# Expert-row gathers of a decoder kernel: their DRAM view, what they wait for, and their place in a step

## The chip, the cores and the metric

The kernel runs on one core of a Trainium2 chip. The metric is the device time of one execution in microseconds (us); lower is better. Times of the kernel before are 1217.22, 1217.5 and 1214.28 us, median 1217.22 us.

## The reference

One decoder layer on x of shape (8, 512, 256), in float32: windowed self-attention with a residual, cross-attention to 64 context rows with a residual, and a last block of a small attention and a mixture of experts. Only the last block touches the change. Its attention runs over the batch of 8 (512 independent positions), and its experts are chosen by arg-max:

```python
def _moe(x, Wg, W1, b1, W2, b2):
    xf = x.reshape(S * B, D)                  # 4096 tokens, D = 256
    idx = jnp.argmax(xf @ Wg.T, axis=-1)      # one of E = 8 experts per token
    out = jnp.zeros_like(xf)
    for e in range(E):
        m = (idx == e)[:, None].astype(xf.dtype)
        h = jax.nn.relu(xf @ W1[e] + b1[e])   # DF = 1024
        out = out + m * (h @ W2[e] + b2[e])
    return out.reshape(S, B, D)
y = _layer_norm(x + _mha(x, ...), g1, be1)
z = _layer_norm(y + _moe(y, Wg, W1, b1, W2, b2), g2, be2)
return x + z
```

## The kernel before, in words

A first part (lines 196 to 692) does the two attentions batch by batch; it ends near 680 us of the profile and is not touched. The second part (from line 704) does the last block and has three kinds of work.

*Blocks.* 4096 tokens are cut into NBLK = 8 blocks of four groups of 128 tokens. `block_start` normalises a block and makes its q, k and v. `group` does the attention of one group: scores (L794, L805), their maximum on VectorE (L814), exponentials on ScalarE (L820), in its next step the reciprocal of the sums (L828, VectorE) and the scaling of the weights (L829, a 128x512 multiply on GpSimd), in the step after that four transposes of the scaled weights on TensorE (L834), then the product with the values (L841) and the projection (L190, L854). `block_end` normalises the block (L154 to L158, L167, L170), transposes it (L179), computes the expert logits (L871, L885), counts how many tokens each expert has seen (L905) and gives each token a row in a DRAM table, `rows_d`, of 8 x 4096 rows of 513 words: the expert's region and the token's rank in it (`sloti`, L911 to L929). Four indirect DMAs issued by GpSimd, one per group, scatter the block's rows there (L931), two in one step and two in the next.

*Tables.* `make_table` runs three times, after blocks 3, 5 and 7. From the counts it derives which full tiles of 128 rows of one expert exist by then: expert index (`eidx`) and source rows (`srci`) per tile. Table t0 holds tiles 0 to 8 (NT1 = 9), t1 tiles 9 to 16 (NT2 = 17), t2 tiles 17 to 38 (NT = 39). t0 takes rows of blocks 0 to 3 only, t1 of blocks 0 to 5, t2 of all.

*Expert tiles.* `expert_tile(i)` gathers 128 rows from `rows_d` by an indirect DMA of GpSimd into one of seven buffers `tb` (L1067; the first seven tiles clear their buffer first, L1064). A step later SyncE loads the expert's first weights, b1 and b2 (L1079, 1 MB, L1081, L1083). A step later the rows are transposed on TensorE (L1094; VectorE copies them out, L1096, and takes the token numbers, L1087), a step later comes the first matmul (L1105, 32 matmuls) with its relu (L1110, L1112) and two additions on GpSimd (L1116, L1117), a step later the second matmul (L1121, 16 matmuls), its statistics and a power on GpSimd (L1135), and a step later the last two VectorE operations (L1137, L1138) and the scatter of the result to the output (L1139, GpSimd). The weights go into buffers that blocks 2 to 5 used for the rows they scattered (tags y2 to y5), so the first loads into such a buffer wait for that block's scatters.

*What sets the order.* `in_steps` (line 70) runs all these works as generators, one piece of each per step, sorted by the rank that the piece before yielded (a new work has the rank with which it is entered): PREFIX 0, TURN 1, VALUES 2, SMALL 3, SCORES 4, OTHER 5, EXPS 6, LOADS 7; at equal rank the newest work comes first. `in_order` (line 51) then ties each of TensorE, VectorE, ScalarE and GpSimd to that order. Block n enters at step 4n and its `block_end` at step 4n + 15; its scatters are in steps 4n + 20 and 4n + 21. Tile i enters at step 34 + i with rank PREFIX, so its gather stands before the multiply L829 of that step, which belongs to a group's piece that also has rank PREFIX but is older. The tiles' transposes L1094 (rank TURN) open TensorE's part of step 36 + i; the group's transposes L834 (SMALL) follow.

*What waits for what.* Dependencies between DMAs and compute are found from the tensors that they name. `dram_disjoint_views` hands out views of one DRAM tensor that count as disjoint from each other, so scatters do not wait for one another. The gather names the whole of `rows_d`, which overlaps every view:

```python
group_rows = dram_disjoint_views(rows_d, NGRP)
...
out=group_rows[n * NG + g0 + g],   # a scatter writes its own view
...
in_=rows_d,                        # a gather reads the whole tensor
```

A gather therefore waits for every scatter that stands before it in the order, and a scatter waits for every gather that stands before it. Both kinds wait in GpSimd's own instruction stream, ahead of everything behind them there. GpSimd's DMAs share eight semaphores in turn, so a DMA also waits for the eighth one before it.

Of the kernel before, what the change touches and what calls it, by code (L numbers as in the profile page):

```python
# [27 lines left out]
NBLK = S // (GP * NG)  # L28
# [3 lines left out]
NGRP = S // GP  # L32
NT = (B * S + E * (P - 1)) // P
NB1, NB2 = 4, 6
# [5 lines left out]
PREFIX, TURN, VALUES, SMALL, SCORES, OTHER, EXPS, LOADS = range(8)  # L40
# [58 lines left out]
def decoder_kernel(ctx: ExitStack, tc: tile.TileContext, a: dict, out: bass.AP):  # L99
    nc = tc.nc  # L100
# [8 lines left out]

    rows_d = dram.tile([E * B * S, ROW], I32, name="rows_d")  # L110

    group_rows = dram_disjoint_views(rows_d, NGRP)
    tile_rows = dram_disjoint_views(out.rearrange("b s d -> (b s) d"), NT)

    cst = const.tile([P, C_N], F32, name="cst")
# [31 lines left out]
    def statistics(src):  # L147

        n = src.shape[1]
        st = small.tile([P, NG, 6], F32, tag="st")  # L150
        mv = small.tile([P, NG, 2], F32, tag="mv")
        rs = small.tile([P, NG], F32, tag="rs")
        for i in range(n):
            nc.vector.bn_stats(st[:, i, :], src[:, i, :])  # L154
        for i in range(n):
            nc.vector.bn_aggr(mv[:, i, :], st[:, i, :])
        nc.vector.tensor_scalar(rs[:, :n], mv[:, :n, 1], EPS, None, ALU.add)  # L157
        nc.gpsimd.tensor_tensor(rs[:, :n], rs[:, :n], nhalf[:, :n], ALU.pow)  # L158
        return mv, rs
# [36 lines left out]
    with ExitStack() as p1:  # L196
# [59 lines left out]
        def context_keys():  # L256
            for hf in range(2):
                ps = ps_m.tile([P, 512], F32, tag="m")
                project(ps, xwk, hf * P, ctxT)
                for r, mask in enumerate((mask_e, mask_o)):  # L260
                    nc.vector.tensor_scalar(
                        kc[:, hf, :, r, :],
                        ps.rearrange("p (b k) -> p b k", k=NKC),
                        xbk[:, hf : hf + 1],
                        mask,
                        ALU.add,
                        ALU.mult,
                    )
                yield

        def context_values(bs):
            for b in bs:
                ps = ps_m.tile([P, 512], F32, tag="m")
                for r in range(2):
                    heads = slice(r * HD, (r + 1) * HD)
                    for k in range(2):
                        nc.tensor.matmul(
                            ps[r * 64 : (r + 1) * 64, :P],
                            ctxT[:, k, b * NKC : (b + 1) * NKC],
                            xwv[:, k, :].rearrange("p (j d) -> p j d", d=2 * HD)[:, :, heads],  # L280
                            start=k == 0,
                            stop=k == 1,
                        )
                for r in range(2):
                    rows = slice(r * 64, (r + 1) * 64)
                    heads = slice(r * HD, (r + 1) * HD)
                    nc.vector.tensor_tensor(
                        vc[rows, b, :, heads],
                        ps[rows, :P].rearrange("p (j d) -> p j d", d=HD),
                        xbv[rows].rearrange("p (j d) -> p j d", d=2 * HD)[:, :, heads],  # L290
                        ALU.add,
                    )
                if b % 2:
                    yield
# [7 lines left out]
        rows = [slice(32 * j, 32 * j + 32) for j in range(4)]  # L302
# [375 lines left out]
        works = [(4, context_keys()), (6, context_values(range(B)))]  # L678
# [25 lines left out]
    with ExitStack() as p2:  # L704
# [151 lines left out]
        def block_end(n, g0, ng):  # L856

            yr = state[n]["yr"]
            y = yr[:, g0 : g0 + ng, :D]
            stats = statistics(y)  # L860
            yield
            normalised(y, y, *stats, g1, be1)
            yield
            yT = fx.tile([P, 2, NG * P], F32, tag="yT", bufs=1, name=f"fyT_{n}_{g0}")
            transposed(yT[:, :, : ng * P], y, ps_m)
            yield

            ps = ps_m.tile([P, P], F32, tag="m")
            for k in range(2):
                for g in range(ng):  # L870
                    nc.tensor.matmul(  # L871
                        ps[32 * g : 32 * g + 32, :],
                        wg[:, k, :],
                        yT[:, k, g * P : (g + 1) * P],
                        start=k == 0,
                        stop=k == 1,
                        skip_group_check=True,
                    )
            lT = fx.tile([P, P], F32, tag="lT", bufs=1, name=f"lT_{n}_{g0}")
            nr = 32 * ng  # L880
            nc.scalar.copy(lT[:nr], ps[:nr])
            yield

            pl = ps_m.tile([P, NG, 32], F32, tag="m")
            nc.tensor.transpose(  # L885
                pl.rearrange("p g e -> p (g e)")[:, :nr], lT[:nr], ident[:nr, :nr]
            )
            lg = pl[:, :ng, :E]
            top = small.tile([P, NG], F32, tag="top")
            rv = small.tile([P, NG, E], F32, tag="lg")  # L890
            mk = small.tile([P, NG, E], F32, tag="emk")
            for i in range(2):
                nc.vector.tensor_reduce(top[:, :ng], lg, AX.X, ALU.max)
                nc.vector.tensor_tensor(
                    mk[:, :ng], lg, top[:, :ng].unsqueeze(2).to_broadcast([P, ng, E]), ALU.is_equal
                )
                if i == 0:
                    rev = cst[:, C_REV : C_REV + E].unsqueeze(1).to_broadcast([P, ng, E])
                    nc.vector.tensor_tensor(rv[:, :ng], mk[:, :ng], rev, ALU.mult)
                    lg = rv[:, :ng]  # L900

            before = small.tile([P, NG + 1, E], F32, tag="seen", bufs=2, name=f"seen{n}_{g0}")
            nc.vector.tensor_copy(before[:, 0], seens[-1])
            for g in range(ng):
                nc.vector.tensor_tensor(before[:, g + 1], before[:, g], mk[:, g, :], ALU.add)  # L905
            seens.append(before[:, ng])
            yield

            pr = ps_m.tile([P, NG, E], F32, tag="m")
            for w, v in ((cst[:, C_LT : C_LT + P], mk), (ones, before)):  # L910
                nc.tensor.matmul(  # L911
                    pr[:, :ng].rearrange("p g e -> p (g e)"),
                    w,
                    v[:, :ng].rearrange("p g e -> p (g e)"),
                    start=v is mk,
                    stop=v is before,
                )
            rk = small.tile([P, NG, E], F32, tag="rk")
            nc.vector.tensor_tensor(
                rk[:, :ng],  # L920
                pr[:, :ng],
                cst[:, C_E4 : C_E4 + E].unsqueeze(1).to_broadcast([P, ng, E]),
                ALU.add,
            )
            nc.vector.tensor_tensor(rk[:, :ng], rk[:, :ng], mk[:, :ng], ALU.mult)
            slot = small.tile([P, NG], F32, tag="slot")
            nc.vector.tensor_reduce(slot[:, :ng], rk[:, :ng], AX.X, ALU.add)
            sloti = small.tile([P, NG], I32, tag="sloti")
            nc.vector.tensor_copy(sloti[:, :ng], slot[:, :ng])  # L929
            for g in range(ng):  # L930
                nc.gpsimd.indirect_dma_start(  # L931
                    out=group_rows[n * NG + g0 + g],
                    out_offset=bass.IndirectOffsetOnAxis(ap=sloti[:, g : g + 1], axis=0),
                    in_=yr[:, g0 + g, :].bitcast(I32),
                    in_offset=None,
                )
                if g == 1:
                    yield

# [7 lines left out]


        tables = []

        def table(name, cnt, op, n, base, ends):

# [100 lines left out]
        def expert_tile(i):  # L1053
# [3 lines left out]
            k = sum(i >= n for n in at) - 1  # L1057
            (eidx, srci, void), j = tables[k], i - at[k]
            if i < 7:
# [7 lines left out]
            nc.gpsimd.indirect_dma_start(  # L1067
                out=t.bitcast(I32),
                out_offset=None,
                in_=rows_d,  # L1070
                in_offset=bass.IndirectOffsetOnAxis(ap=srci[:, j : j + 1], axis=0),
                bounds_check=E * B * S - 1,
                oob_is_err=False,
            )
            yield LOADS
            e_sp = nc.sync.value_load(eidx[0:1, j : j + 1], min_val=0, max_val=E - 1)
            w1 = fy.tile([P, NG, ROW], F32, tag=f"y{2 + i % 3 if i < 7 else (2, 5, 3, 4)[i % 4 - 2]}", name=f"w1_{i}")
# [42 lines left out]
            for f in range(NFC):  # L1120
# [21 lines left out]
                in_=r,  # L1142
# [6 lines left out]
        works = [(9, expert_weights())]  # L1149
# [5 lines left out]
        for k, (nb, n) in enumerate(((NB1, NT1), (NB2, NT2 - NT1), (NBLK, NT - NT2))):  # L1155
            works.append((4 * nb + 16, make_table(f"t{k}", n, nb < NBLK)))
        for i in range(NT):
            works.append((4 * NB1 + 18 + i, expert_tile(i), PREFIX))
        with in_order(tc):
            in_steps(works)  # L1160

# [102 lines left out]
```

## Time and profile before

| | |
|---|---|
| median of three runs | 1217.22 us (1214.28 to 1217.5) |
| the profiled execution's own time | 1219.89 us |
| its span, first to last instruction | 1218.1 us |
| TensorE (PE) busy | 1100.2 us, 90% |
| VectorE (DVE) / ScalarE (ACT) / GpSimd (POOL) busy | 722.7 / 581.8 / 498.7 us |
| mean granted TensorE clock | 0.953 |
| chain that ended last | PE 64%, DVE 18%, ACT 8%, issue 3%, DMA 3%, POOL 3% |
| scatters into `rows_d` (L931) | 32, 780.2 to 1015.4 us, median 0.972 us of GpSimd each |
| gathers from `rows_d` (L1067) | 9 + 8 + 22, from 870.0, 951.2 and 1025.5 us, median about 1.07 us each |

The page is read in this order: busy time and clock by engine, the slices that show where an engine thins out, then the chain that ended last, and from there the waits and the timeline of the stretch in question. Times in a timeline are microseconds from the start of the span. A releaser is what ended an idle time; where a wait had several conditions it is the one that the profile saw last, so one whose engine had long been done stands for another, often a DMA.

### The profile page before, as it was taken

The page shows a single profiled execution, that of the slowest core. Times are in us where ns is not written, and L with a number is a line of the kernel's source. Part 1 is how long each engine was busy: PE and PEld are TensorE (multiplying, and loading weights), DVE is VectorE, ACT ScalarE, POOL GpSimd, SP SyncE. Part 2 cuts the span into 40 slices and gives each one's busy share as a digit, 9 for nine tenths or more (in the row PEclk, how much of TensorE's full clock was granted, in tenths as well). Part 3 has the DMA queues.
Part 4 walks back from the last instruction along what each step waited for, and adds up shares of the span by engine and source line. Part 5 has one row for each costly group of instructions (what it writes and reads, how often), then busy time and mean ns, then how long its engine had stood idle before and what let it go on. Part 6 is the DMA issues. An engine that isn't in the chain of part 4 may idle for free.

```text
span 1218.1 us, 24488 instructions
## 1 busy us (share of the span) xinstructions
PE 1100.2 (90%) x8900; PEld 793.9 (65%) x8900; DVE 722.7 (59%) x1830; ACT 581.8 (48%) x2037; POOL 498.7 (41%) x580
## 2 busy tenths in 40 slices
PE   6798998999989999899876699999789999999995
PEld 3455666566655666656553367766568988999994
DVE  2947758477584866848551336667547764544553
ACT  2866758576595765867701165555332111111110
POOL 2242524425244243431510233544455566555543
PEclk9997999999999999999987699999899989999998
DMA  5000001010010100100001760120345866666630
GB/s 192 1 1 5 7 1 45 1 40 6 1 45 2 39 6 11 35 2 27 2 18 46 209 204 1 36 70 36 137 131 193 274 215 196 225 195 204 213 128 7
DMA packets 60727, 97.66 MB, mean 80 GB/s; under 512 B 15930, under 2 KB 43965, under 8 KB 60608
## 3 DMA queue, kind: packets, MB, share of 16 engines
q1 hardware_dynamic: 53056, 75.08, 19.9%
q0 software_dynamic: 7552, 21.02, 5.0%
q8 instruction: 72, 1.18, 0.4%
q14 instruction: 47, 0.39, 0.1%
HBM read 81.12 MB, written 17.71 MB: 81 GB/s over the span
## 4 chain that ended last, share of the span: by engine, by line
PE 64%; DVE 18%; ACT 8%; issue 3%; DMA 3%; POOL 3%; SPq 0%; POOLq 0%; DVEq 0%
PE ps L185 12%; PE ps L190 11%; PE hps L1105 9%; PE ps L1121 9%; ACT s L449 5%; PE sc L402 2%; DVE nm L445 2%; DVE s L429 2%; PE xav L636 2%; DVE nm L578 2%; PE ps L179 2%; DMA rows_d<-y,sloti 2%; PE av L507 2%; PE ps L805 1%; DVE kg L362 1%
## 5 line engine op out<-in xcount | busy, mean ns | idle before, releaser
L449 ACT ACTIVATE s<-s,nm 128x144 f32<-128x144 f32 (+1 forms) x512 | 203.7, 408 | 11.4 <-DVE nm L445 11.4
L1110 ACT ACTIVATE h<-hps,b 128x128 f32<-128x128 f32 x156 | 44.6, 369 | 233.7 <-issue 188.6
L1105 PE MATMUL hps<-tT,w 128*128 128x128 f32 x1248 | 150.2, 280 | 0.7 <-issue 0.6
L1105 PEld LDWEIGHTS hps<-tT,w 128*128 128x128 f32 x1248 | 146.7, 196 | 2.0 <-issue 0.6
L1121 PE MATMUL ps<-w,h 128*128 x624 | 141.0, 379 | 0.0
L484 POOL TENSOR_TENSOR pc<-pT,cst 128x512 f32<-128x512 f32 x96 | 122.8, 1300 | 24.9 <-DVE pT L480 24.7
L1121 PEld LDWEIGHTS ps<-w,h 128*128 128x128 f32 x624 | 115.7, 190 | 14.1
L449 ACT ACTIVATION_READ_ACCUMULATOR s<-s,nm 128x1 f32 x512 | 100.8, 197 | 0.0
L460 POOL COPY rx<-s 128x128 f32<-128x128 f32 x48 | 14.7, 306 | 193.5 <-ACT s L449 193.5
L445 DVE TENSOR_REDUCE nm<-s 128x8 f32<-128x1152 f32 (+1 forms) x64 | 84.5, 1320 | 13.2 <-POOL s L438 9.4
L1112 DVE TENSOR_SCALAR h<-hps,b 128x128 f32<-128x128 f32 x156 | 43.9, 344 | 65.0 <-ACT h L1110 58.0
L402 PE MATMUL sc<-kz,qT 32*128 32x512 f32 (+1 forms) x512 | 76.1, 603 | 4.1 <-DVE s L421 3.0
L429 DVE COPY_PREDICATED s<-upto_q,sc 128x512 f32<-128x512 int32 x96 | 64.8, 729 | 24.6 <-ACT s L428 24.5
L478 PE MATMUL pt<-cst,s 128*128 128x128 f32 x512 | 72.4, 281 | 2.6 <-ACT pT L482 1.1
L158 POOL TENSOR_TENSOR rs<-rs,nhalf 128x4 f32<-128x4 f32 x32 | 33.4, 1043 | 95.5 <-DVE rs L157 95.4
L478 PEld LDWEIGHTS pt<-cst,s 128*128 128x128 f32 x512 | 60.5, 145 | 15.3 <-issue 7.1
L428 ACT COPY s<-sc 128x512 f32<-128x512 f32 x96 | 51.6, 590 | 37.6 <-PE sc L402 37.5
L185 PE MATMUL ps<-fxT,w_fwqkv 128*128 128x512 f32 x128 | 60.9, 621 | 0.0
L463 DVE RECIPROCAL rc<-sm 128x8 f32<-128x8 f32 x64 | 12.6, 197 | 80.8 <-ACT s L449 80.8
L185 PE MATMUL ps<-xT,w_wqkv 128*128 128x512 f32 x128 | 58.5, 599 | 0.0
L829 POOL TENSOR_TENSOR s<-s,sm 128x512 f32<-128x512 f32 x32 | 33.4, 1045 | 59.0 <-DVE sm L828 56.7
L1139 POOL DMA_INDIRECT out<-r,to x39 | 39.8, 1020 | 29.5 <-DVE r L1138 13.4
(241 smaller groups left out, 2297.7 us busy)
## 6 DMA issues: line engine op xcount, KB each, us to landing
w<-in_W SPq DMA_DIRECT2D x47, 1024.0 KB
b<-in_b SPq DMA_DIRECT2D x39, 128.0 KB
xb<-in_x SPq DMA_DIRECT2D x8, 512.0 KB
x2d<-xb SPq DMA_DIRECT2D x8, 512.0 KB
y<-x2d SPq DMA_DIRECT2D x32, 128.0 KB
mi<-in_mask SPq DMA_DIRECT2D x8, 128.0 KB
mj<-in_maskT SPq DMA_DIRECT2D x8, 128.0 KB
w_wqkv<-in_wqkv SPq DMA_DIRECT2D x1, 768.0 KB
```

The source lines that it names most:

```text
L185: nc.tensor.matmul(ps, w[:, k, o0 : o0 + P], xT[:, k, :], start=k == 0, stop=k == 1)
L190: nc.tensor.matmul(ps, xT[:, k, t0 : t0 + P], w[:, k, o0 : o0 + D], start=k == 0, stop=k == 1)
L402: nc.tensor.matmul(ps[j // 2][:, j % 2].rearrange("p r w k -> p r (w k)"), qT[rows[j], hf, q0 : q0 + P], kz[rows[j], hf, :, q0 + P - nw * ...
L428: nc.scalar.copy(s4, ps[jj][:, :, :, 0, :])
L429: nc.vector.copy_predicated(s4, upto_q.unsqueeze(1).unsqueeze(1).to_broadcast([P, 2, 2, P]), ps[jj][:, :, :, 1, :],)
L445: nc.vector.tensor_reduce(nm, s[:, :, :nk], AX.X, ALU.max, negate=True)
L449: nc.scalar.activation(s[:, h, :nk], s[:, h, :nk], AF.Exp, bias=nm[:, h : h + 1], accum_out=sm[:, h : h + 1],)
L478: nc.tensor.transpose(pt[:, h, :], s[:, 4 * jj + h, :P], ident)
L484: nc.gpsimd.tensor_tensor(pc[:, hs, :], pT[:, hs, :], upto_k.unsqueeze(1).to_broadcast([P, 4, P]), ALU.mult,)
L1105: nc.tensor.matmul(ps[:, f, :], w1[:, k, f * P : (f + 1) * P], tT[:, k, :], start=k == 0, stop=k == 1)
L1110: nc.scalar.activation(h[:, f, :], ps[:, f, :], AF.Relu, bias=b1[:, f : f + 1])
L1121: nc.tensor.matmul(ps, h[:, f, :], w2[:, bass.ds(e_pe, 1), f, :].rearrange("p o d -> p (o d)"), start=f == 0, stop=f == NFC - 1,)
```

## The change

The gathers get views of their own, one per tile, that count as disjoint from the scatters' views and from each other. What a gather has to wait for is then said by name: the first 16, 24 or 32 scatters for a tile of table t0, t1 or t2. The instruction list is searched for the scatter just issued, and its name kept. Tiles enter their first step with rank VALUES in place of PREFIX.

```diff
-    group_rows = dram_disjoint_views(rows_d, NGRP)
+    group_rows = dram_disjoint_views(rows_d, NGRP + NT)
...
                     in_=yr[:, g0 + g, :].bitcast(I32),
                     in_offset=None,
                 )
+                scatters.append(traced()[-1].name)
...
         tables = []
+        scatters = []
+
+        def traced():
+            return nc.cur_bb.bb.instructions
+
+        known = (4 * NB1, 4 * NB2, 4 * NBLK)
...
             nc.gpsimd.indirect_dma_start(
                 out=t.bitcast(I32),
                 out_offset=None,
-                in_=rows_d,
+                in_=group_rows[NGRP + i],
                 in_offset=bass.IndirectOffsetOnAxis(ap=srci[:, j : j + 1], axis=0),
...
             )
+            gather = traced()[-1]
+            for scatter in scatters[: known[k]]:
+                tc.add_manual_dep(
+                    gather,
+                    scatter,
+                    mybir.DependencyInfo(mybir.DependencyClass.Sync, mybir.DependencyReason.DATA),
+                    reason="rows",
+                )
             yield LOADS
...
         for i in range(NT):
-            works.append((4 * NB1 + 18 + i, expert_tile(i), PREFIX))
+            works.append((4 * NB1 + 18 + i, expert_tile(i), VALUES))
```

In the built programs TensorE, VectorE, ScalarE and SyncE have the same instructions in the same order before and after. GpSimd has the same instructions; in each of steps 34 to 39 (865 to 913 us of the profile) the multiply L829 stands ahead of the clearing of `tb` and the gather (tiles 0 to 5), where it stood behind them, and nothing else changes place. Of the conditions on GpSimd's instructions, the scatters lose the gathers and the gathers the scatters that their table does not count; what is left of that kind is the first gather of each table, which waits for the last scatters that it counts, and the turn of the eight semaphores.

## The prediction

> **What bounds the kernel now.** I read the waits of TensorE (PE) first, between 840 and 1030 us, the stretch in which blocks 4 to 7 and the first expert tiles run side by side. PE is 90% busy over the span, and after 1030 us a tile takes 7.25 us with no gap (L1094 at 1034.20, 1041.44, 1048.69 in its timeline), so a gain can only lie in this stretch. Columns: who waited, for whom, us in total, times, longest.
>
> ```profile
> PE pt L834 <- POOL s L829: 10.4, 3, 5.1
> PE pt L1094 <- DMA tb<-rows_d,t1srci: 5.2, 2, 2.6
> ```
>
> PE waits for GpSimd's multiply and for two gathers. GpSimd's timeline (start, length; idle before it and its releaser in brackets) says why the multiply and the gathers are late:
>
> ```profile
> 864.76 0.97 POOL L931 DMA_INDIRECT rows_d<-y,sloti  x1 [0.30 <-issue]
> 865.74 0.54 POOL L1064 MEMSET tb<- 128x513 f32 x1
> 870.00 1.07 POOL L1067 DMA_INDIRECT tb<-rows_d,t0srci  x1 [3.72 <-DMA rows_d<-y,sloti]
> 871.10 1.05 POOL L829 TENSOR_TENSOR s<-s,sm 128x512 f32<-128x512 f32 x1
> ...
> 894.77 1.05 POOL L1067 DMA_INDIRECT tb<-rows_d,t0srci  x1 [4.23 <-DVE to L1087]
> ...
> 978.10 0.97 POOL L931 DMA_INDIRECT rows_d<-y,sloti  x1 [3.16 <-DMA tb<-rows_d,t1srci]
> ...
> 985.24 1.07 POOL L1067 DMA_INDIRECT tb<-rows_d,t1srci  x1 [2.94 <-DMA rows_d<-y,sloti]
> ```
>
> A multiply stands behind a gather that waits for scatters just issued; later, scatter waits for gather and gather for scatter, in turn. (The 4.23 us names VectorE, but this gather waits for the two scatters of 887.67 and 889.03; the second landed at 893.97 in the trace's semaphore records.) PE's timeline shows the four gaps:
>
> ```profile
> 872.20 1.11 PE L834 MATMUL pt<-cst,s 128*128 128x128 f32 x4 [5.08 <-POOL s L829]
> 896.95 1.11 PE L834 MATMUL pt<-cst,s 128*128 128x128 f32 x4 [4.46 <-POOL s L829]
> 989.17 0.66 PE L1094 MATMUL pt<-cst,tb 128*128 128x128 f32 x2 [2.63 <-DMA tb<-rows_d,t1srci]
> 1024.65 0.41 PE L1094 MATMUL pt<-cst,tb 128*128 128x128 f32 x2 [2.57 <-DMA tb<-rows_d,t1srci]
> 1025.46 5.44 PE L1105 MATMUL hps<-tT,w 128*128 128x128 f32 x32 [0.40 <-issue]
> ```
>
> Each gap has a second price. In the windows view (stretch, its us, busy us of PE, PEld, DVE, ACT, POOL, then clock, DMA share, GB/s) the clock is 0.50 after it:
>
> ```profile
> 869.20:872.60 3.40, 0.40 (x2) 0.40 (x3) 0.00 (x0) 0.00 (x0) 2.57 (x3) 0.50 0.55 180
> 872.60:876.05 3.45, 3.45 (x23) 2.15 (x22) 0.00 (x0) 2.17 (x10) 2.12 (x3) 0.50 0.86 319
> 893.10:896.50 3.40, 0.00 (x0) 0.00 (x0) 1.58 (x7) 0.35 (x2) 1.70 (x2) 1.00 0.00 0
> 896.50:899.94 3.44, 2.99 (x28) 2.04 (x28) 0.00 (x0) 1.31 (x5) 1.63 (x3) 0.50 0.25 76
> 988.70:992.10 3.40, 2.93 (x14) 2.96 (x15) 2.91 (x8) 0.00 (x0) 2.90 (x4) 0.50 0.47 76
> 992.10:995.50 3.40, 3.40 (x18) 3.40 (x17) 3.19 (x12) 0.00 (x0) 3.18 (x5) 0.50 0.98 380
> 1026.20:1029.65 3.45, 3.45 (x19) 3.45 (x18) 2.87 (x10) 0.00 (x0) 3.11 (x4) 0.51 0.86 264
> ```
>
> Half of PE's busy time in a slow stretch is lost. So gap A (5.08) costs 5.1 + 3.8/2 = 7.0 us, B 4.5 + 3.0/2 = 6.0, C 2.6 + 6.3/2 = 5.8, D 2.6 + 0.4 + 3.45/2 = 4.7: together 23.5 us, the most that this stretch can give.
>
> **What the Trainium skill says.** "TensorE: Matmul & The Clock Gate", Part 1, What's actually happening: an idle window of about 3.4 us puts PE at half its clock, a busy one releases it, on a window that runs freely. The trace agrees: slow stretches of 3.4 or 6.8 us at 0.50 behind each gap. "DMA: Bandwidth & Descriptors", Anatomy of one DMA — SWDGE (gpsimd) path: the wait for a semaphore sits in the issuing sequencer, and most of the fixed 2 us is the write's receipt, slowest to HBM. It agrees in kind: the scatter of 864.76 keeps GpSimd for 0.97 us and landed at 869.18, 4.4 us after its start. Same page, Queues, rings and completion order: each DMA engine takes its queues in turn, packet by packet. In the trace gather 0, issued at 870.00 half a microsecond behind a 1 MB weight load, landed only at 875.72, against 3.5 us for gather 2 (880.49 to 883.97).
>
> **The change, part by part.** In the built order only GpSimd changes: in steps 34 to 39 the multiply stands ahead of the clearing and the gather. Count, kind and length of all instructions stay, so nothing is added on any engine; the views and names exist only at build time.
>
> *Gap A: it moves.* The multiply's reciprocal L828 was ready at 864.05 (VectorE, 863.88 + 0.17), so it runs at 865.74 and PE goes on at 867.1 without a gap. But gather 0 may not move: it still needs all 16 scatters of blocks 0 to 3, and the last of them (864.76) landed at 869.18; it issues at 870.0 and lands at 875.7 as before. What is late next is PE's transpose of tile 0 (L1094, 877.03 before, no wait). PE's step before it takes some 3.1 us at full clock (863.33 to 865.42 for L834 to L805, then 1.0 for L885 and L190), so PE stands from 870.2 to 875.7, 5.5 us, and the half clock follows from there to 879.46 or 882.87. I replayed the next two steps. Step 36 has 4.4 us of work and ScalarE wait at full clock; at half clock it ends near 881.4, before at 881.47. Step 37 loses its wait of 0.85 us for the multiply, but L179 in it waits for VectorE's chain, which starts from L805, 0.3 to 1.1 us sooner than before. Net of gap A at L1094 of tile 2: +1.1 us if the clock recovers at 879.46, 0 if at 882.87. I take +0.5; bounds -1 and, if gather 0 didn't hold PE at all, +7.
>
> *Gap B: gone.* The multiply of step 37 (895.85 before) stood behind gather 3, which waited for two scatters. Now it follows the scatters at about 888.8 and is done near 889.9; PE wants it at 892.1 less the shift of about 1, at 891. Gain 6.0. Gather 3 no longer waits either: 890.7, landed near 894.3, wanted by PE after 900.
>
> *What comes next behind B.* Block 4's last scatters go out at 893.3 in place of 899.73, so the third weight load (1 MB, 903.78 before, waiting for them) starts at about 897.3. Before, it landed at 910.47 (6.7 us; three loads followed one another), and its matmul began at 910.54. It would land by 904.0; PE wants it at 910.54 less about 7, 903.5. I charge 0.4 (bounds 0 and 1). Later loads are ahead by 4 us or more (the one for tile 7: 945.98, landed 951.14, used at 955.63).
>
> *Gaps C and D: gone.* Gather 12 (985.24) waits for the scatters at 979.37, these for gather 11 (972.55), this for the scatters at 966.88. Without this chain GpSimd has per step a gather 1.1, an output scatter 1.0, two scatters 2.0, L1116 and L1117 1.4, a power 0.6 and some 1.0 of issue, about 7.1 us, within PE's 7.25 to 8, so the queue keeps up: gather 12 goes out near 975, lands near 980 and is wanted at 986.4. The same holds for gather 16 (D). Table t2's chain on VectorE (992.87 to 998.34) delays block 7's `sloti` and with it GpSimd, by some 5 us; gathers are issued two steps, some 15 us, ahead of their use and land in 4 to 6, which covers it. Gain 5.8 + 4.7 = 10.5 us.
>
> *Moved gathers.* Six gathers stand one multiply later, 1.05 us on GpSimd each; behind them only the clearing and that step's scatters. Cost nothing: GpSimd is idle for 9.1 us (850 to 860) and 5.0 us (before 887.67) in this stretch; without that cover it would be 6 x 1.05 = 6.3 us on the scatters, not on PE. The first gathers of t1 and t2 wait for scatters that landed a step earlier: nothing.
>
> Sum: 0.5 + 6.0 - 0.4 + 5.8 + 4.7 = 16.6 us. The profiled execution (1219.89 us, span 1218.1 and 1.8 around it) would come to 1203.3; the median lies 2.7 us under it, and I put the gain on the median: 1217.2 - 16.6 = 1200.6.
>
> **Rivals.** *All four gaps close*: if gather 0 lands soon enough, 1217.2 - 23.5 = 1193.7. For: gather 2's 3.5 us. Against: the same weight load is released by the same scatters, half a microsecond ahead. *C and D come back as other waits*: for: L1138 waits 34.3 us in all for GpSimd's power in this stretch, so GpSimd's queue may be late by its own work of 7.1 us a step and by VectorE's table; one gap of 5.8 or 4.7 stays and B is worth less: about 1208. Against: the replay above, with 4 us to spare. *The change doesn't do what it says*, some wait keeps scatters and gathers tied: 1217; the built conditions show them gone. *Slower*: the six moved gathers wait behind a multiply that waits for its reciprocal in VectorE's order, and come too late for their transposes. Steps 35 to 37 last some 4.4 to 7 us, two of them 9 at least, and a gather needs 1.05 + 5.7; if a multiply starts more than about 2 us into its step, PE waits at L1094, at gap C's price of 5.8 us. Six such gaps are 35 us, against 16.6 gained: 1236; three or more already end slower. Against: the reciprocals of steps 34 and 35 are ready at 864.05 and 867.67, before GpSimd gets there.
>
> **How the numbers follow.** Measurement can tell about 0.3% (3.7 us) from no change. Main case 1200.6: 0.63, its own range 1197 to 1204. All gaps close: 0.11. Some of C and D stays: 0.17, 1204 to 1212. Nothing: 0.04. Slower: 0.05. The range reaches from 1194.5 to 1208.5. Faster by over 0.3%: 0.91.
>
> **What would show it.** After the change PE's waits should have no L834 behind L829 of over 1 us, one L1094 of about 5 us behind a gather of t0 near 876 us with the clock at 0.50 behind it, and none behind t1; the mean clock rises above 0.953; GpSimd's scatters have no releaser that is a gather, and only the first gather waits for a scatter; L1138's wait for L1135 shrinks. I am wrong if L1094 waits in several of steps 36 to 41, if L1105 waits for its weights for more than 1 us, or if gather 0 lands before 872 us.

## The result, and the profile after

The changed kernel takes 1197.12 us, the median of six runs (1195.67 to 1200.58), against 1216.51 for the kernel before in six runs (1212.47 to 1218.51) on the same chip. The ratio is 0.985, with a 95% interval of 0.983 to 0.987: faster by 18.1 us (1.5%) by this ratio, 19.4 us by the medians, where the prediction had 16.6 and a time of 1200.6. The profiled execution took 1196.64 us, its span 1194.9 us, its mean clock 0.966. In the changed file lines after the edits stand lower: L829 is now L830, L834 is L835, L1067 is L1075, L1094 is L1110, L1105 is L1121, L1138 is L1154.

Read in the same order as before, the longest wait of PE between 840 and 1030 us (who waited, for whom, us in total, times, longest) in the changed kernel is:

```profile
PE pt L1110 <- DMA tb<-rows_d,t0srci: 5.5, 1, 5.5
```

The next in the list is 1.5 us in all. The wait for the multiply (10.4 us before) and the waits for gathers of t1 (5.2 before) have left the list; one wait for a gather of t0 is new. GpSimd's timeline of the changed kernel shows why:

```profile
859.00 0.96 POOL L932 DMA_INDIRECT rows_d<-y,sloti  x1 [0.31 <-PE av L842]
859.98 1.06 POOL L830 TENSOR_TENSOR s<-s,sm 128x512 f32<-128x512 f32 x1
...
864.06 1.09 POOL L1075 DMA_INDIRECT tb<-rows_d,t0srci  x1 [2.55 <-DMA rows_d<-y,sloti]
...
885.03 1.09 POOL L1075 DMA_INDIRECT tb<-rows_d,t0srci  x1 [0.27 <-POOL tb L1072]
```

The multiply stands directly behind the scatter. Gather 0 still waits for the scatters, but the multiply of its step no longer stands behind it. Gather 3 (885.03), which had waited for two fresh scatters, waits only for the clearing of its buffer. In the list of GpSimd's waits in the same stretch the kernel before has six waits of gathers for scatters, 15.3 us in all, and scatters that wait for gathers, 10.2 us:

```profile
POOL tb L1067 <- DMA rows_d<-y,sloti: 15.3, 6, 3.7
...
POOL rows_d L931 <- DMA tb<-rows_d,t1srci: 7.4, 2, 4.2
...
POOL rows_d L931 <- DMA tb<-rows_d,t0srci: 2.8, 2, 1.5
```

In the changed kernel one wait of a gather for scatters is left, and no scatter is listed as waiting for a gather:

```profile
POOL tb L1075 <- DMA rows_d<-y,sloti: 2.6, 1, 2.6
```

PE's timeline shows the places of the four gaps:

```profile
861.20 0.60 PE L835 MATMUL pt<-cst,s 128*128 128x128 f32 x4
870.03 0.66 PE L1110 MATMUL pt<-cst,tb 128*128 128x128 f32 x2 [5.54 <-DMA tb<-rows_d,t0srci]
...
886.09 0.60 PE L835 MATMUL pt<-cst,s 128*128 128x128 f32 x4
...
974.04 0.38 PE L1110 MATMUL pt<-cst,tb 128*128 128x128 f32 x2
...
1003.70 0.38 PE L1110 MATMUL pt<-cst,tb 128*128 128x128 f32 x2
```

Gap A has moved from L834 to the transpose of tile 0 and is 5.54 us long; B, C and D have no bracket left. The windows view (columns as in the prediction) has half clock behind the moved gap, and the clock records have none from 877.10 to 1184 us, where B, C and D lay:

```profile
863.45:866.86 3.41, 1.03 (x5) 0.58 (x4) 3.32 (x12) 0.82 (x6) 2.60 (x3) 1.00 0.66 192
866.86:870.27 3.41, 0.24 (x2) 0.27 (x3) 2.36 (x12) 0.00 (x0) 2.90 (x3) 0.50 0.88 310
870.27:873.68 3.41, 2.68 (x16) 1.72 (x15) 0.42 (x1) 0.77 (x2) 1.82 (x3) 0.50 0.18 28
873.68:877.10 3.42, 3.42 (x16) 2.66 (x14) 1.86 (x4) 1.59 (x9) 0.00 (x0) 0.50 0.13 53
877.10:880.50 3.40, 2.67 (x29) 1.93 (x28) 3.19 (x11) 1.39 (x5) 0.00 (x0) 1.00 0.00 0
```

**One anchor for both traces.** The spans differ by 23.2 us, more than the medians. To see what belongs to the change, take as zero the start of the first scatter of block 3: nothing before it is edited. It is at 859.73 us before and at 853.97 after. So 5.8 us of the 23.2 lie in a first part that has the same instructions in both kernels, where the clock records show 81.9 us at half clock before and 61.4 after. In the other profiles of kernels with the same first part this start lies between 852.1 and 857.6; the profile of the kernel before had a late one. From the anchor to the end of the span it is 358.4 us before and 340.9 after, 17.4 us less. All that follows uses this number, called "the rest" below, beside the timed ratios. The transposes of single tiles, in us from the anchor:

| tile | before | after | gained since the row above | what lies between |
|---|---|---|---|---|
| 2 | 32.4 | 31.9 | 0.5 | gap A |
| 3 | 48.3 | 41.8 | 6.0 | gap B |
| 11 | 119.3 | 112.7 | 0.1 | weight loads |
| 13 | 140.4 | 128.0 | 5.8 | gap C |
| 17 | 174.5 | 157.0 | 5.1 | gap D |

### The profile page after: what moved, and what is told of

The parts are those of the page before. It is cut to its first block, busy times and chain, and to the rows that moved or that the text cites. A ratio compares the mean times of both kernels' runs of the same rounds, so it can differ in the third digit from the quotient of the medians.

```text
span 1194.9 us, 24487 instructions
## 1 busy us (share of the span) xinstructions
PE 1084.9 (91%) x8900; PEld 784.3 (66%) x8900; DVE 722.3 (60%) x1830; ACT 580.4 (49%) x2037; POOL 498.7 (42%) x580
## 4 chain that ended last, share of the span: by engine, by line
PE 70%; DVE 16%; ACT 6%; DMA 2%; POOL 2%; issue 1%; SPq 0%; POOLq 0%; DVEq 0%; ACTq 0%
PE ps L186 12%; PE hps L1121 11%; PE ps L191 11%; PE ps L1137 11%; ACT s L450 4%; DVE nm L446 2%; DVE s L430 2%; PE sc L403 2%; PE xav L637 2%; DVE nm L579 2%; PE ps L180 2%; PE pt L479 2%; PE ps L806 2%; PE av L508 1%; DVE kg L363 1%; PE xk L601 1%
## 5 line engine op out<-in xcount | busy, mean ns | idle before, releaser
L1121 PE MATMUL hps<-tT,w 128*128 128x128 f32 x1248 | 146.1, 275 | 0.1
L1121 PEld LDWEIGHTS hps<-tT,w 128*128 128x128 f32 x1248 | 142.9, 192 | 0.7 <-issue 0.3
L830 POOL TENSOR_TENSOR s<-s,sm 128x512 f32<-128x512 f32 x32 | 33.4, 1042 | 59.5 <-DVE sm L829 57.3
L1151 POOL TENSOR_TENSOR rs<-rs,nhalf 128x1 f32<-128x1 f32 x39 | 22.8, 586 | 76.0 <-DVE to L1105 57.9
## 6 DMA issues: line engine op xcount, KB each, us to landing
b<-in_b SPq DMA_DIRECT2D x39, 128.0 KB
y<-x2d SPq DMA_DIRECT2D x32, 128.0 KB
mi<-in_mask SPq DMA_DIRECT2D x8, 128.0 KB
mj<-in_maskT SPq DMA_DIRECT2D x8, 128.0 KB
```

Of the source, the lines that this page charges most:

```text
L1121: nc.tensor.matmul(ps[:, f, :], w1[:, k, f * P : (f + 1) * P], tT[:, k, :], start=k == 0, stop=k == 1)
```

## The experiments

Each edit is made to the changed kernel unless it says otherwise. The ratio is to the kernel before, timed on the same chip, with its 95% interval.

**Each half of the change alone.** First only the place in the step, in the kernel before:

```diff
-            works.append((4 * NB1 + 18 + i, expert_tile(i), PREFIX))
+            works.append((4 * NB1 + 18 + i, expert_tile(i), VALUES))
```

> The kernel before with the rank VALUES alone; gathers still name the whole table. My theory (the gain comes from the waits that the names remove, the place in the step only moves gap A and closes gap B): gap A turns into a wait of tile 0's transposes of 5 to 6 us, gap B goes, but the third weight load, which still starts only after block 4's last scatters have waited for gather 3, holds its matmul by 3 to 5 us, and C and D stay. 1211 to 1215 us, 2 to 5 under before. Rival (the place in the step does it, because the multiply no longer stands behind a waiting gather): A and B both gone, 1203 to 1206.

Measured: 1218.61 us, ratio 1.0008 (0.9999 to 1.0018); no gain, so the expected 2 to 5 us were missed, though the waits are those that were expected. PE's timeline of this kernel:

```profile
870.44 0.66 PE L1094 MATMUL pt<-cst,tb 128*128 128x128 f32 x2 [5.69 <-DMA tb<-rows_d,t0srci]
...
903.26 5.46 PE L1105 MATMUL hps<-tT,w 128*128 128x128 f32 x32 [3.77 <-DMA w<-in_W]
...
983.31 0.66 PE L1094 MATMUL pt<-cst,tb 128*128 128x128 f32 x2 [2.41 <-DMA tb<-rows_d,t1srci]
```

Gap A has moved, C stands as before, and so does D (3.04 us at 1019.30). Gap B is gone, and with A's 0.5 its 6.0 us are there at tile 3 (41.8 us from the anchor), but nothing of them is left at tile 11 (119.1, before 119.3): PE now waits 3.8 us for a weight load, and the 32 matmuls behind it run at half clock for a part, 5.46 us against 3.73 in the changed kernel. The expectation had the wait without this second part. That load goes into a buffer that block 4 scattered from, and in this kernel two of these scatters still wait for gather 3, and gather 3 for the two scatters before it. The gain of B was turned into another wait.

Then only the views and names:

```diff
-            works.append((4 * NB1 + 18 + i, expert_tile(i), VALUES))
+            works.append((4 * NB1 + 18 + i, expert_tile(i), PREFIX))
```

> The changed kernel with rank PREFIX as before: views and names, no move. Theory: TensorE waits 5 us for the multiply behind gather 0 as before (gap A in its old place), B shrinks to under 1 us since gather 3 no longer waits, C and D are gone: 1197 to 1200, within 2 us of the changed kernel. Rival (the move is needed for B): B stays at 3 us or more with its slow clock, 1202 to 1205.

Measured: 1199.53 us, ratio 0.985 (0.983 to 0.986), the rest 342.3 us: as expected, all but 1.3 us of the change. PE's longest wait is gap A at its old place:

```profile
PE pt L835 <- POOL s L830: 6.4, 3, 5.2
```

So B, C and D are closed by the names; the place in the step only decides which instruction stands in gap A.

**Which kind of wait.** The change removed scatters waiting for gathers and gathers waiting for scatters. The first run lets each gather wait for all earlier scatters again; the second lets each scatter wait for all earlier gathers (whose names are kept in `gathers`).

```diff
-            for scatter in scatters[: known[k]]:
+            for scatter in scatters:
```

> The changed kernel with each gather told to wait for all scatters that stand before it, as in the kernel before; scatters still wait for no gather. Theory (gaps C and D need both kinds of wait in turn, about 10 us a step on GpSimd; one kind alone adds 2 to 3 us to a step of 7, which the gathers' lead of two steps covers; gap B comes back in part as a wait for tile 2's weights of 2 to 3 us): ratio 0.986 to 0.989. Rival (each kind of wait is enough to keep C and D): ratio 0.993 or more.

```diff
                 scatters.append(traced()[-1].name)
+                for gather in gathers:
+                    tc.add_manual_dep(
+                        traced()[-1],
+                        gather,
+                        mybir.DependencyInfo(mybir.DependencyClass.Sync, mybir.DependencyReason.DATA),
+                        reason="rows",
+                    )
```

> The other half: gathers wait for the scatters that their table counts alone, but each scatter is told to wait for all gathers that stand before it, as in the kernel before. Theory, as for the other half: no gap C or D, a wait for tile 2's weights of 1 to 3 us, ratio 0.985 to 0.988. Rival: ratio 0.993 or more.

Measured: with waiting gathers 1208.21 us, ratio 0.994 (0.992 to 0.996), the rest 354.2; with waiting scatters 1203.87 us, 0.991 (0.989 to 0.994), the rest 343.9. Both are slower than expected: my theory, that the gathers' lead of two steps covers one kind of wait, fell. The rival, that each kind is enough to keep C and D, is met by its number with waiting gathers, but there only D comes back. PE's waits with waiting gathers:

```profile
PE pt L1110 <- DMA tb<-rows_d,t0srci: 5.7, 1, 5.7
PE pt L1110 <- DMA tb<-rows_d,t1srci: 3.7, 1, 3.7
...
PE hps L1121 <- DMA w<-in_W: 2.9, 1, 2.9
```

and with waiting scatters, where L1110 and L1121 stand at L1119 and L1130:

```profile
PE pt L1119 <- DMA tb<-rows_d,t0srci: 5.7, 1, 5.7
PE hps L1130 <- DMA w<-in_W: 1.5, 1, 1.5
...
PE pt L1119 <- DMA tb<-rows_d,t1srci: 1.2, 1, 1.2
```

Waiting gathers bring back gap D (the wait for t1, at 1016.85) and the wait for weights, while C stays closed (tile 12 follows tile 11 by 7.4 us). Waiting scatters bring the wait for weights and a small gap at a gather of t1. The full gain needs both kinds removed. The profiles fit the timed runs only roughly: that with waiting gathers is of the slowest of six executions, and that with waiting scatters has a rest only 3.0 us over the changed kernel's, where the ratio stands for 7 to 8 us. What the other executions lose there is not shown.

**The gap that is left: later tiles.** Gap A stands because tile 0's transpose is wanted before its gather lands. If every tile enters one step later, PE has other work in that step:

```diff
-            works.append((4 * NB1 + 18 + i, expert_tile(i), VALUES))
+            works.append((4 * NB1 + 19 + i, expert_tile(i), VALUES))
```

> The changed kernel with all expert tiles entered one step later. Theory (what is left in the stretch is gap A alone: gather 0 lands 5.7 us after its issue, and its transposes come two short steps later): with a third step in between, the wait of 5.5 us falls to about 1 us and the half clock of 10 us behind it goes; the work of TensorE is the same, so nothing is paid back: 1188 to 1192. Rival (each step that the tiles start later is a step of 7.25 us that they end later): 1197 to 1204.

With `20 + i`, two steps:

> The same with two steps. Theory: no wait at all at tile 0's transposes, 1187 to 1191, within 2 us of one step later. Rival: two steps of 7.25 us later, or tiles too few to fill the steps 41 to 49, so that VectorE and GpSimd hold TensorE there: 1198 or more.

Measured: one step later 1193.38 us, ratio 0.980 (0.979 to 0.982), the rest 336.6 and 6.8 us at half clock in place of 10.2; a little above the expected time, and the rest is 4.3 us shorter than with the change alone. The wait that is left was expected at about 1 us and is 2.0:

```profile
PE pt L1110 <- DMA tb<-rows_d,t0srci: 2.0, 1, 2.0
```

Two steps later 1197.36 us, 0.983 (0.981 to 0.984), the rest 339.1: worse than one step, and not the expected 1187 to 1191. PE's wait for gather 0 is down to 0.8 us, but PE waits for the multiply, 4.0 us in two waits, the longer one at 878.46. GpSimd's timeline of that kernel:

```profile
875.05 1.01 POOL L932 DMA_INDIRECT rows_d<-y,sloti  x1 [3.11 <-DVE sm L829]
...
877.36 1.05 POOL L830 TENSOR_TENSOR s<-s,sm 128x512 f32<-128x512 f32 x1
```

Block 4's scatters wait for `sloti` at the end of a chain on VectorE (L930 at 874.60; the L829 that the bracket names comes directly behind it), and the multiply stands behind them. So closing the gap further only brings up the next wait; the profile does not show how the 0.8 and 4.0 us share the 2.5 us by which two steps are longer than one.

**The gap that is left: a faster gather.** Gather 0 takes 5.83 us to land (864.06 to 869.89 in the trace's semaphore records), gather 2 takes 3.5. Gather 0 shares the DMA engines with a 1 MB weight load. Here tile 1's load waits for gather 0 (its name is kept as above):

```diff
+            if i == 1:
+                tc.add_manual_dep(
+                    traced()[-1],
+                    gathers[0],
+                    mybir.DependencyInfo(mybir.DependencyClass.Sync, mybir.DependencyReason.DATA),
+                    reason="load",
+                )
```

> The changed kernel with one wait more: the 1 MB weight load of tile 1, which the same scatters release as gather 0, is told to wait for gather 0. Theory (gather 0 lands 5.8 us after its issue because that load fills the DMA engines' queues half a microsecond before it): gather 0 lands about 3.5 us after its issue, TensorE's wait for it falls from 5.5 to about 3.3 us and its half clock from 10 to about 7: 3 to 4 us under the changed kernel, a ratio of 0.981 to 0.983 to the kernel before. Rival (the first gather is slow by itself): the wait stays at 5.5 us, ratio 0.985.

And together with the later step:

> Both: tiles one step later, and tile 1's weight load behind gather 0. Theory: the 2.0 us that TensorE still waited for gather 0 go, and the half clock of 6.8 us behind them with it or by half: 2 to 5 us under one step later alone, ratio 0.976 to 0.979. Rival (gather 0's landing isn't the load's doing, or something else in those short steps is as late): ratio 0.980.

Measured: alone 1196.75 us, ratio 0.985 (0.983 to 0.988); with the later step 1193.41 us, 0.982 (0.981 to 0.984). Both are above the expectation. The mechanism is there: gather 0 lands 3.45 us after its issue (867.29 to 870.74), and PE waits for it 3.0 us in place of 5.5 (L1119 is the transposes' line in this kernel):

```profile
PE pt L1119 <- DMA tb<-rows_d,t0srci: 3.0, 1, 3.0
```

So tile 2 comes 3.0 us sooner after the anchor, and the rest is 338.1 us, 2.8 less than in the first profile of the change. But the timed runs do not separate it from the changed kernel. With the later step the rest is 336.6 us, no less than for the later step alone, although no half clock follows the anchor before the tail of the span. PE then waits for the multiply (L835 for L830), 3.1 us in two waits, and the load that was held back lies beside gather 1, which lands 5.3 us after its issue in place of 3.5. Tile 2 stands 30.4 us behind the anchor in both kernels: with the load held back, the waits for the multiply take the place of the wait for gather 0 and of its half clock.

**All four on one chip.** To compare the versions with each other, the changed kernel, one step later and both edits ran again beside the kernel before (1218.21 us), with no new edit:

> The changed kernel once more, on the same chip as the three that follow, so that they can be set against it: ratio 0.985 to the kernel before; from the first scatter of block 3 to the end of the span 341 us, as in its first profile.

> One step later, beside the changed kernel on one chip. Theory (gap A is what is left, and it costs time): 4 to 6 us under the changed kernel, 336.6 us from block 3's first scatter to the end. Rival (the first difference came from the chip it ran on): within 2 us.

> One step later and tile 1's weight load behind gather 0. In the first profiles both variants took 336.6 us from block 3's first scatter to the end, since the multiply takes the place of gather 0 as the last to come. So: within 1.5 us of one step later alone, 4 to 6 us under the changed kernel. Rival (its lower ratio in the other set was real): 2 us or more slower than one step later alone.

Measured: the changed kernel 1197.34 us, ratio 0.982 (0.979 to 0.986); one step later 1193.71, 0.979 (0.976 to 0.982); both edits 1193.15, 0.979 (0.976 to 0.982). The later step is 3.6 us under the changed kernel by the medians and 4.4 by the ratios, each of its runs under each of the changed kernel's, and holding the load back adds nothing that can be told. The rest is 336.7 and 336.6 us, as in the first runs. For the changed kernel it is 344.7 here, 3.8 more than in its first profile, for which PE's waits give the reason:

```profile
PE pt L1110 <- DMA tb<-rows_d,t0srci: 6.2, 1, 6.2
PE hps L1121 <- DMA w<-in_W: 1.6, 1, 1.6
```

In this execution of the changed kernel the third weight load comes too late, and a slow stretch of 3.41 us follows it. The load is issued 0.85 us later after the anchor than in the first profile and takes 7.18 us to land in place of 5.05; why is not shown.

**The place in the step, with later tiles.** The last run, in the same group, takes the later step with the old place:

```diff
-            works.append((4 * NB1 + 18 + i, expert_tile(i), VALUES))
+            works.append((4 * NB1 + 19 + i, expert_tile(i), PREFIX))
```

> One step later with rank PREFIX, so that a gather stands ahead of the multiply again. Theory (with gather 0 no longer awaited two short steps later, what the place in the step decides is whether the multiply of step 35 stands behind gather 0's own wait for block 3's scatters): TensorE waits 3 to 5 us for that multiply, with 3 to 7 us of half clock behind it: 3 to 6 us slower than one step later with the move, as fast as the changed kernel or 2 us faster. Rival (the place doesn't matter, as it didn't without the later step): within 1.5 us of one step later.

Measured: 1198.75 us, ratio 0.984 (0.981 to 0.987), the rest 342.9 us: 5.0 us over the same step with the new place, as expected, with 10.2 us at half clock where 3 to 7 were expected. PE waits again for the multiply:

```profile
PE pt L835 <- POOL s L830: 6.8, 2, 4.5
```

The order of multiply and gather is worth little where another wait of 5.5 us takes the place of the one it removes (the names alone against the whole change), and 5 us where only one of some 2 us is left.

## Why the prediction was right

*Gap A moves.* Right in place and length, and within its bounds in price. Predicted: PE stands 5.5 us at tile 0's transpose, net gain 0.5 at tile 2. Measured: 5.54 us, and 0.5. Gather 0 is issued 10.1 us after the anchor (10.3 before) and lands at 15.9 (16.0 before), so its landing did not move. The clock took the longer of the two courses, half clock from 866.86 to 877.10, 10.2 us. For that course the prediction had a gain of 0; its 0.5 lay between the two courses, so that the price is met to the tenth is luck. The warning "gather 0 lands before 872" is met by the letter, at 869.89, but only because the whole stretch begins 5.8 us earlier; the sign should have been given from an anchor.

*Gap B.* Predicted 6.0, measured 6.0 between tiles 2 and 3. That it stays gained is due to the names: with the place alone the weight load took it back.

*The third weight load.* Charged 0.4 with bounds of 0 and 1; a wait of over 1 us at L1105 was named as a sign of being wrong. In the first profile it cost nothing (L1121 starts at 898.28 without a wait); in the second it cost a wait of 1.57 us and 1.73 us for half clock (5.46 us for the 32 matmuls in place of 3.73), 3.3 us together, of the 3.8 by which that profile is longer. This term was mis-sized: its upper bound should have been some 3 us, since a half-clocked stretch can follow such a wait. It need not: with waiting scatters the matmuls behind a wait of 1.5 us took 3.84 us.

*Gaps C and D.* Predicted 5.8 and 4.7, measured 5.8 and 5.1. GpSimd keeps up, as the count of 7.1 us per step said: VectorE's wait of L1138 (L1154 now) for GpSimd's power fell to a third, before and after:

```profile
DVE r L1138 <- POOL rs L1135: 33.2, 8, 9.0
DVE r L1154 <- POOL rs L1151: 11.5, 7, 3.2
```

The two runs on the kinds of wait show that both belong to the cause: either one left in costs a part of the gain.

*Moved gathers.* Charged nothing, and no transpose but tile 0's waits for a gather. With the later step the move even gains 5 us, because it takes the gather out of the multiply's way.

The sum of 16.6 stands against 17.4 from the anchor in the first profile, 13.7 in the second, and 18.1 by the timed ratio. The mean clock rose from 0.953 to 0.966, as one of the signs said, but mostly for another reason: of 31.1 us less at half clock 20.5 lie ahead of the anchor. None of the rivals came true in the changed kernel; other waits in the place of gaps are seen with either half of the waits left in, and at the third weight load in the second profile. That all gaps close did not happen; the later step comes nearest to it (336.6, 21.8 us less than before), and at 1193.4 and 1193.7 us it is faster than both kernels, and no other version is measurably faster than it.

Two more things stay open. Why holding the load back shortens the profile by 2.8 us and not the timed runs is not settled; the intervals of some 0.2% either way would hide 2.6 us. And in how many executions the third weight load is late is not known: it is late in one of two profiles.

## What to carry to other kernels

If DMAs that write and read one DRAM tensor share an in-order instruction stream, list what each really needs and look at who stands behind the one that waits: here the waits that nothing needed cost 18 us, and leaving either direction in gave back four to six tenths of it. A wait that is moved rather than removed brings nothing by itself; ask which buffer or load it delays next. Compare profiles from a common anchor ahead of the edit, since the part in front of it can differ by several us without any cause in the change.

## What the runs showed of the hardware

- An indirect gather of 128 rows of 513 words (gather 0) landed 5.57 to 6.27 us after its issue in the ten profiles in which a 1 MB load had been issued 0.6 us before it, and 3.45, 3.50 and 3.54 us after it in the three in which that load was held back. The Trainium skill, "DMA: Bandwidth & Descriptors", Queues, rings and completion order, says that a DMA engine takes its queues in turn, packet by packet; the landing times agree with that, and the changed kernel with the load held back and without give the price here: 2.4 us.
- The clock fell to half behind a window that was not wholly idle: PE was busy for 1.03 us of 863.45 to 866.86 and went idle only at 864.49, and the next three windows ran at 0.50. The Trainium skill, "TensorE: Matmul & The Clock Gate", Part 1, What's actually happening, speaks of an idle window of about 3.4 us. The length agrees (the stretches are multiples of 3.41 us), but here PE was 30% busy in the window that ended in half clock, and the third slow window followed one in which it was busy for 2.68 of 3.41 us; the measurement decides. The other profiles bear it out. Between 700 and 1150 us of all fourteen there are 23 drops to half clock, and in the 3.41 us ahead of each PE was busy for 0 to 1.86 us. Of the full-clock windows with at most 1.57 us busy none was without a drop behind it, and of those with 1.59 to 1.94 us some were.
